# Order of the row loads of two engines in a graph layer: four rows a turn, semaphores in program order

## Chip, cores and metric

The kernel runs on one core of one Trainium2 chip. The metric is device time in microseconds of that core, the median of several runs.

## What is computed

A pre-norm graph layer with a residual, on 12500 nodes of 128 features and 200000 edges that are sorted by their target `dst`. All arrays are float32. Cut to what matters:

```python
z = relu(layernorm(x))                                # 12500 x 128
agg = segment_sum(z[src], dst) / max(deg, 1)          # deg: edges that end at a node
h = relu(agg @ Wg + z @ Ws + bg)                      # 128 -> 128
h = tanh(h @ W1 + b1)                                 # 128 -> 512
h = tanh(h @ W2 + b2)                                 # 512 -> 512
out = x + h @ W3 + b3                                 # 512 -> 128
```

## The kernel before

**Start.** The normalised rows of `x` are computed and written to a table `htab` in device memory (one row is 512 bytes). The indices are transposed, so that column `c` of `scol` holds the 128 sources of chunk `c`, and `dloc` their targets relative to a window of target nodes.

**Chunks.** The 200000 edges are 1563 chunks of 128 edges. Since the edges are sorted by target, a chunk's targets lie with near certainty in a window of 144 nodes around 8c. For a chunk, `add(c)` (L432) lets PE multiply the 128 gathered rows by a one-hot matrix `oh` (made by DVE for 8 chunks together, L382, with its column counts `cnt`, L392), which adds each row to its target's column of a PSUM accumulator `agg`. Chunks whose window reaches over two blocks are added in `edge`, copied out by ACT (`sums`) and merged by two further products. If an edge lay outside its window, a flag would send the program to a general version, which is not run here.

**Rows of a chunk** come in one of three ways:

- 1437 chunks by an indirect transfer of POOL from `htab` into one of 32 buffers (`gather`, L308). Up to 32 are asked for ahead of PE.
- 80 chunks (`raw`, 8 in each 40 from chunk 256 on to chunk 656) directly from `x`, at the start of the kernel, normalised afterwards in SBUF.
- 46 chunks (`slow`) by 128 single transfers of one row each, with the row's address from a register: 27 chunks (`slow_s`) by SP into the tiles `srows`, and 19 (`slow_a`) by ACT into `arows`. This is `row_loads` (L337), a generator: for 32 rows the addresses are loaded into registers, then 32 transfers are issued, and at each `yield` it hands back to the main loop. ACT's stops after four rows, SP's after 32. Each of the two has four tiles.

**Blocks.** The target nodes form blocks of 512 (64 chunks), smaller at the end. For block `b` the layers (`part0` to `part4`) follow when its chunks are added. `own` (L480) asks SP for the block's rows of `htab` (`hb`), and `own_turned` (L489) lets PE turn them by four transposes (`pt`) into `hT`, which ACT copies out. `own_part` asks SP for the rows of `x` (`xb`). `part4` leaves the result `o`, which `store` lets SP write out twelve chunks later (`LATE`), and without a delay from chunk 1376 (`QUICK`) on.

**Order.** The main loop runs over all chunks. PE's products, ACT's operations and the transfers of SP and ACT are kept in program order on their own engine by `tc.keep_in_program_order` (helpers at L297, L300, L306, L329, L332, L335). All else, the order between two engines included, is set by the scheduler, which lays all instructions out in one order by its estimate of their times. In that order the transfers of SP and ACT get eight completion semaphores in turn. A transfer waits until all earlier ones of its semaphore are done.

In the main loop the turn of the row loads is set by `behind`, the number of chunks gathered by POOL that have been passed:

```python
        if not raw(c) and c not in slow:
            behind += 1
            batch = behind * P // (EACH * LOADS)               # EACH = 48, LOADS = 32
            if behind > SLOW0 - 3 * EACH and batch > (behind - 1) * P // (EACH * LOADS):
                next(loading, 0)                               # SP: 32 rows each 12 chunks
            batch = behind * P // (EACH_A * TOGETHER)          # EACH_A = 60, TOGETHER = 4
            if behind > 48 and batch > (behind - 1) * P // (EACH_A * TOGETHER):
                next(loading_a, 0)                             # ACT: four rows each 1.9 chunks
```

A chunk loaded by rows is complete some 100 chunks before it is used. At `c % 64 == 54` come `own_turned` of the next block and right behind it `own` of the one after, so that `hb` is asked for 64 chunks ahead of its use.

Of the kernel before, what the change touches and what calls it, by code (L numbers as in the profile page):

```python
# [31 lines left out]
P = 128  # L32
# [9 lines left out]
SLOW0 = 160  # L42
EACH = 48
EACH_A = 60
TOGETHER = 4
LOADS = 32
# [14 lines left out]
def windowed(ctx, tc, x, src, dst, Wg, Ws, bg, W1, b1, W2, b2, W3, b3, out, flag):  # L61
    nc = tc.nc
# [19 lines left out]
    def raw(c):  # L82
        return RAW0 <= c < RAW1 and (c - RAW0) % STEP < GRP


    slow_s, slow_a = [], []
# [47 lines left out]
    for t, a in ((rsrc, src), (rdst, dst)):  # L134
        a = a[RAW0 * P : RAW1 * P].rearrange("(u e) -> u e", u=NRAW)[:, : GRP * P]
# [46 lines left out]
    def centre(pool, xt, k, stats):  # L182
        nc.vector.tensor_reduce(stats[:, 0], xt, AX.X, ALU.add)
        nc.vector.scalar_tensor_tensor(xt, spread(stats[:, 0], k), -1.0 / D, xt, op0=ALU.mult, op1=ALU.add)
        sq = pool.tile([P, k, D], F32, name=f"sq{k}")
        nc.scalar.activation(sq, xt, AF.Square)
        nc.vector.tensor_reduce(stats[:, 1], sq, AX.X, ALU.add)

    def factors(stats):
        nc.scalar.activation(stats[:, 1], stats[:, 1], AF.Sqrt, bias=eps, scale=1.0 / D)  # L190
        nc.vector.reciprocal(stats[:, 1], stats[:, 1])
# [110 lines left out]
    def flat(t):  # L302
        return t.rearrange("p a b -> p (a b)")

    def sp_dma(*a):
        tc.keep_in_program_order(nc.sync.dma_start(*a))  # L306

    def gather(c):  # L308
        r = rows_in.tile([P, D], F32, name="rows")
        nc.gpsimd.indirect_dma_start(  # L310
            out=r, out_offset=None, in_=htab,
            in_offset=bass.IndirectOffsetOnAxis(ap=scol[:, c : c + 1], axis=0),
        )
        rows_t[c] = r
# [10 lines left out]
    class act:  # L325
# [6 lines left out]
            tc.keep_in_program_order(nc.scalar.copy(*a))  # L332

        def dma(*a):
            tc.keep_in_program_order(nc.scalar.dma_start(*a))  # L335

    def row_loads(chunks, engine, dma, name, together):  # L337
        for c in chunks:
            i = slow.index(c)
            r = rows_one.tile([P, D], F32, name=name)  # L340
            rows_t[c] = r
            rb = r.bitcast(U8)
            for p0 in range(0, P, LOADS):
                loads, vs = nc.values_load_multi_w_load_instructions(  # L344
                    place[i : i + 1, p0 : p0 + LOADS], engines=[engine], min_val=0, max_val=(N - 1) * ROWB,
                    skip_runtime_bounds_check_because="src holds rows of x, as the indirect DMAs take it to",
                )
                for ld in loads:
                    tc.keep_in_program_order(ld)
                for p, v in enumerate(vs, p0):  # L350
                    dma(rb[p : p + 1, :], hbytes[bass.ds(v, ROWB)].rearrange("(o b) -> o b", o=1))
                    if (p + 1) % together == 0:
                        yield

    def raw_stats(i):
        return stats_raw[:, :, i * GRP : (i + 1) * GRP]

    def raw_scaled(i):
        h = raw_rows[i]
        scale(h, h, GRP, raw_stats(i))  # L360
        for j in range(GRP):
            rows_t[RAW0 + i * STEP + j] = h[:, j]
# [11 lines left out]
    def onehot(g):  # L374
        k = min(GRP, NCH - g * GRP)
        lo, w = window(g * GRP)
        is_raw = raw(g * GRP)
        oh = ed.tile([P, GRP, W_RAW], F32, name="ohr", bufs=2) if is_raw else oh_bufs[g % OHS]
        if not is_raw and w < oh_w[g % OHS]:
            nc.vector.memset(oh[:, :, w : oh_w[g % OHS]], 0.0)  # L380
            oh_w[g % OHS] = w
        nc.vector.tensor_tensor(  # L382
            oh[:, :k, :w], lane[:, None, :w].to_broadcast([P, k, w]),
            dloc[:, g * GRP : g * GRP + k][:, :, None].to_broadcast([P, k, w]), op=ALU.is_equal,
        )
        ohs[g] = oh
        step, n = (oh.shape[2], w) if is_raw else (PITCH - per, w + per * (k - 1))
        cnt = ed.tile([P, PITCH], BF16, name="cnt", bufs=16)
        part, row, col = oh.ap
        shifted = bass.AP(tensor=oh.tensor, offset=oh.offset, ap=[part, [col[0], n], [step * col[0], k]])  # L390
        with nc.allow_low_precision(reason="whole numbers up to the chunks of a group"):
            nc.vector.tensor_reduce(cnt[:, :n], shifted, AX.X, ALU.add)  # L392
        counts[g] = (lo, n, cnt)
# [10 lines left out]
    def count(b):  # L404

        n, m = blocks[b]
        dg = flat(ps_m.tile([P, 4, P], F32, name="pm"))
        groups = sorted({c // GRP for c in reach[b]})
        for g in groups:
            lo, w, cnt = counts[g]  # L410
            a0, a1 = max(lo, n), min(lo + w, n + m)
            pe.matmul(
                dg[:, a0 - n : a1 - n], ones, cnt[:, a0 - lo : a1 - lo], start=(g == groups[0]), stop=(g == groups[-1]),
                skip_group_check=True,
            )
        rd = ml.tile([P, BLK], F32, name="rd", bufs=3)
        nc.vector.tensor_scalar(rd[:, :m], dg[:, :m], 1.0, None, op0=ALU.max)  # L417
        nc.vector.tensor_reduce(total[:, b : b + 1], dg[:1, :m], AX.X, ALU.add)
        nc.vector.reciprocal(rd[:, :m], rd[:, :m])  # L419
        rds[b] = rd  # L420
# [189 lines left out]
        )  # L610

    order = [c for c in range(NCH) if not raw(c) and c not in slow]
    loading = row_loads(slow_s, mybir.EngineType.SP, sp_dma, "srows", LOADS)
    loading_a = row_loads(slow_a, mybir.EngineType.Activation, act.dma, "arows", TOGETHER)
    work, done, nxt, behind = [], 0, 0, 0
    ngrp = -(-NCH // GRP)
# [3 lines left out]
    def store(upto):  # L620
        while stores and stores[0][0] <= upto:
            sp_dma(*stores.pop(0)[1:])

    def soonest():
        two = work[: 2 if len(work) > 1 and work[1][3] < work[0][3] and work[0][4] else 1]
        return min(two, key=lambda w: max(w[2], now), default=None)
# [16 lines left out]
    for c in range(NCH):  # L643
        g = c // GRP
        at = c
        store(c if c >= QUICK else c - LATE)
        if c % GRP == 0 and g + 2 < ngrp:
            onehot(g + 2)
            if raw((g + 2) * GRP):
                raw_scaled(((g + 2) * GRP - RAW0) // STEP)  # L650
            if 2 <= g < 2 + NRAW:
                centre(ed, raw_rows[g - 2], GRP, raw_stats(g - 2))
            if g == 2 + NRAW:
                factors(stats_raw)

        while c % GRP == GRP // 2 and counted < len(blocks) and reach[counted][-1] // GRP <= g + 1:
            count(counted)
            counted += 1
        while nxt < len(order) and nxt < behind + AHEAD:
            gather(order[nxt])  # L660
            nxt += 1
        if not raw(c) and c not in slow:
            behind += 1
            batch = behind * P // (EACH * LOADS)
            if behind > SLOW0 - 3 * EACH and batch > (behind - 1) * P // (EACH * LOADS):
                next(loading, 0)
            batch = behind * P // (EACH_A * TOGETHER)
            if behind > 48 and batch > (behind - 1) * P // (EACH_A * TOGETHER):
                next(loading_a, 0)
        if c >= QUICK:  # L670

            there = 7.5 + 1.251 * (NRAW * GRP + order.index(c)) if c not in slow else 0
            while soonest() and max(now, soonest()[2]) < there:
                go_on(soonest())
            now = max(now, there) + 0.27
        add(c)

        lead = LEAD if c < QUICK else 2
        if done < len(blocks) and (c - lead if across[done] else c) >= reach[done][-1]:
            if across[done]:  # L680
                merge(done)
            quick = reach[done][-1] + LEAD >= QUICK

            before = done - 1 if done and reach[done - 1][-1] + LEAD < QUICK else None
            work.append([layers(done, before), 0, 0, 0, quick and blocks[done][1] <= P])
            done += 1

        if c % span == span - 10 and (c // span + 1) * BLK < N:
            own_turned(c // span + 1)
            if (c // span + 2) * BLK < N:  # L690
                own(c // span + 2)
        if c < QUICK:
            if c % 2 == 0:
                go_on(work[0] if work else None)
        if c == QUICK:
            for b, (_, n) in enumerate(blocks):
                if n < BLK:
                    own_part(b)
# [379 lines left out]
```

## Time and profile before

| | |
|---|---|
| runs (us) | 2780.86, 2771.82, 2799.8; median 2780.86 |
| profiled execution | 2780.86 us; span 2778.6 us from the first to the last instruction |
| mean clock of PE that was granted | 0.743 |
| busy, share of the span | PE 48%, PEld 32%, DVE 38%, ACT 8%, POOL 52% |
| POOL, gathers | 1437 of 945 ns each; first at 114.6 us, last at 2728.2 us |
| SP, row transfers | 3456; first at 117.0 us, last at 2654.4 us |
| ACT, row transfers | 2432; first at 217.8 us, last at 2330.1 us |
| PE, first and last chunk added | 118.0 and 2762.6 us |

Times are from one execution, and lines named L are lines of the kernel. SPq and ACTq are the engines as issuers of transfers; an issuing instruction does not count as busy, so SP has no busy time on the page. PEld is PE's load of the stationary operand, which runs beside its products. A line of waits reads: who waited, for whom, microseconds in total, times, longest. A line of the timeline reads: start, length, what, how many merged, and in brackets the idle time before it and what ended that.

### The profile page before, as it was taken

Reading aid. Unit: us, or ns where it says so; the run is one execution under the profiler, and the core shown is the slowest. Engines: PE = TensorE matmul, PEld = TensorE weight load, DVE = VectorE, ACT = ScalarE, POOL = GpSimd, SP = SyncE. Lnnn points to the kernel's source line nnn. Section 1 sums busy time; section 2 is a strip of 40 time slices with the busy share of each in tenths; the row PEclk is TensorE's granted clock in tenths of the full one; section 3 lists DMA queues with packets and bytes.
Section 4 is the critical chain, followed back from the end, with each engine's and each line's share of the span. In section 5 each row is a group of like instructions: output and inputs, shape, how many; then the busy total and the mean of one; then the engine's idle time right before and its main releaser. Section 6 shows DMA issues by size and latency. Waiting matters only on the chain. (4 is left out here: it accounts for less than half of the span.)

```text
span 2778.6 us, 27033 instructions
## 1 busy us (share of the span) xinstructions
PE 1321.2 (48%) x5212; PEld 886.9 (32%) x5212; DVE 1068.0 (38%) x651; ACT 228.0 (8%) x362; POOL 1437.0 (52%) x1525
## 2 busy tenths in 40 slices
PE   0233535445546564653525534355454453357167
PEld 0122323334324342332313323233232332224147
DVE  6834534254335343442414333243332432224141
ACT  1100100001000000000000000000000000001012
POOL 7666456554555444555526454364544545346261
PEclk9995767777767777786757777676676776678588
DMA  7511111111112111111111111111111111112120
GB/s 185 151 46 50 39 47 47 46 42 43 45 42 52 42 47 44 50 49 42 48 34 50 38 47 42 40 51 39 47 42 41 50 41 45 35 44 51 37 59 23
DMA packets 130516, 139.83 MB, mean 50 GB/s; under 512 B 35940, under 2 KB 105230, under 8 KB 130144
## 3 DMA queue, kind: packets, MB, share of 16 engines
q0 software_dynamic: 48544, 99.52, 14.2%
q1 hardware_dynamic: 73678, 33.92, 4.4%
q10 hardware_dynamic: 8116, 4.59, 0.7%
q14 instruction: 135, 1.11, 0.1%
q8 instruction: 43, 0.70, 0.1%
HBM read 125.07 MB, written 12.82 MB: 50 GB/s over the span
## 5 line engine op out<-in xcount | busy, mean ns | idle before, releaser
L310 POOL DMA_INDIRECT rows<-htab,scol x1437 | 1358.6, 945 | 1266.1 <-PE edge L297 441.5
L297 PE MATMUL pm<-h,w 128*128 128x512 f32 (+4 forms) x1344 | 732.0, 644 | 442.9 <-ACT h L329 237.1
L382 DVE TENSOR_TENSOR oh<-shared,dloc 128x1152 f32<-128x1152 f32 (+2 forms) x186 | 244.1, 1318 | 1203.8 <-PE edge L297 532.8
L392 DVE TENSOR_REDUCE cnt<-oh 128x200 bf16<-128x1600 f32 (+2 forms) x186 | 523.0, 2817 | 5.3
L297 PEld LDWEIGHTS agg<-oh,rows 128*128 128x128 f32 x2070 | 395.1, 236 | 323.4 <-issue 291.4
L297 PE MATMUL agg<-oh,rows 128*128 128x144 f32 (+3 forms) x2070 | 423.5, 336 | 76.0 <-issue 52.0
L297 PEld LDWEIGHTS pm<-h,w 128*128 128x128 f32 x1344 | 246.7, 226 | 478.2 <-ACT h L329 247.1
L300 PE MATMUL pt<-ident,hb 128*128 128x128 f32 x98 | 25.9, 409 | 543.2 <-DMA hb<-htab 480.3
L300 PEld LDWEIGHTS pt<-ident,hb 128*128 128x128 f32 x98 | 17.1, 208 | 548.1 <-issue 548.1
L297 PEld LDWEIGHTS edge<-oh,rows 128*128 128x128 f32 x804 | 146.3, 219 | 116.2 <-issue 113.5
L297 PE MATMUL edge<-oh,rows 128*128 128x144 f32 (+2 forms) x804 | 158.8, 316 | 16.9 <-issue 12.5
L329 ACT ACTIVATE h<-pm,b2c 128x512 f32<-128x512 f32 (+4 forms) x112 | 70.9, 633 | 722.8 <-DMA arows<-htab 224.2
L297 PE MATMUL pm<-mT,wg 128*128 128x512 f32 (+4 forms) x56 | 42.0, 843 | 143.8 <-DVE mT L533 91.5
L329 ACT ACTIVATE h<-pm,b1c 128x512 f32<-128x512 f32 (+4 forms) x112 | 69.8, 632 | 303.1 <-DMA arows<-htab 129.8
L589 DVE TENSOR_TENSOR o<-pt,xb 128x512 f32<-128x512 f32 x23 | 15.9, 691 | 202.7 <-PE pt L300 72.5
L153 POOL DMA_INDIRECT raw<-in_x_dram,rsrc x80 | 77.5, 969 | 25.4 <-issue 24.1
L297 PE MATMUL agg<-sums,ident 128*128 128x140 f32 (+4 forms) x108 | 25.3, 370 | 121.9 <-ACT sums L332 78.2
L419 DVE RECIPROCAL rd<-rd 128x512 f32<-128x512 f32 (+4 forms) x28 | 81.8, 2920 | 0.0
L417 DVE TENSOR_SCALAR rd<-pm 128x512 f32<-128x512 f32 (+4 forms) x28 | 17.4, 620 | 132.5 <-remote 61.8
L297 PEld LDWEIGHTS agg<-sums,ident 128*128 128x128 f32 x108 | 19.2, 243 | 126.2 <-ACT sums L332 79.8
L297 PEld LDWEIGHTS pm<-mT,wg 128*128 128x128 f32 x56 | 11.7, 259 | 148.1 <-DVE mT L533 94.2
L332 ACT COPY hT<-pt 128x512 f32<-128x512 f32 (+1 forms) x25 | 14.4, 578 | 541.4 <-PE pt L300 490.9
(72 smaller groups left out, 526.7 us busy)
## 6 DMA issues: line engine op xcount, KB each, us to landing
srows<-htab SPq DMA_DIRECT2D x3456, 0.5 KB
arows<-htab ACTq DMA_DIRECT2D x2432, 0.5 KB
rows<-htab,scol POOLq DMA_INDIRECT x1437
hb<-htab SPq DMA_DIRECT2D x24, 256.0 KB
xb<-in_x_dram SPq DMA_DIRECT2D x23, 256.0 KB
out_dram<-o SPq DMA_DIRECT2D x23, 256.0 KB
htab<-h SPq DMA_DIRECT2D x6, 896.0 KB
xt<-in_x_dram SPq DMA_DIRECT2D x5, 896.0 KB
```

What stands on the lines that cost most here:

```text
L153: nc.gpsimd.indirect_dma_start(out=t[:, j, :], out_offset=None, in_=x, in_offset=bass.IndirectOffsetOnAxis(ap=rsrc[:, g, j : j + 1], axis=0),)
L297: tc.keep_in_program_order(nc.tensor.matmul(*a, **k))
L300: tc.keep_in_program_order(nc.tensor.transpose(*a, **k))
L310: nc.gpsimd.indirect_dma_start(out=r, out_offset=None, in_=htab, in_offset=bass.IndirectOffsetOnAxis(ap=scol[:, c : c + 1], axis=0),)
L329: tc.keep_in_program_order(nc.scalar.activation(*a, **k))
L332: tc.keep_in_program_order(nc.scalar.copy(*a))
L382: nc.vector.tensor_tensor(oh[:, :k, :w], lane[:, None, :w].to_broadcast([P, k, w]), dloc[:, g * GRP : g * GRP + k][:, :, None].to_broadcas ...
L392: nc.vector.tensor_reduce(cnt[:, :n], shifted, AX.X, ALU.add)
L417: nc.vector.tensor_scalar(rd[:, :m], dg[:, :m], 1.0, None, op0=ALU.max)
L419: nc.vector.reciprocal(rd[:, :m], rd[:, :m])
L589: nc.vector.tensor_tensor(o[:, :whole], po[:, :whole], xb[:, :whole], op=ALU.add)
```

## The change

A helper `in_turn` takes the place of `tc.keep_in_program_order` for the transfers of `sp_dma` and of `act.dma`. Besides keeping each engine's own order it ties each transfer to the one before it in the program, on whichever of the two engines that was. The tie holds for the order in which the scheduler lays the instructions out, and so for the handing out of the semaphores; it adds no wait of its own. It covers the row loads of both engines and, on SP, `hb`, `xb`, the small blocks' rows of `x`, and the stores.

SP's row loads stop after each four rows (`TOGETHER`), and the loop takes a turn at two of three gathered chunks instead of at each twelfth. The address loads stay at 32 rows. The number of chunks, of rows, and the pace of rows per chunk stay.

```diff
+    turn = []
+
+    def in_turn(start):
+
+        tc.keep_in_program_order(start)
+        if turn:
+            tc.add_manual_dep(
+                start.ins, turn.pop(),
+                mybir.DependencyInfo(mybir.DependencyClass.NoSync, mybir.DependencyReason.DATA), reason="in_turn",
+            )
+        turn.append(start.ins.name)
+
     def sp_dma(*a):
-        tc.keep_in_program_order(nc.sync.dma_start(*a))
+        in_turn(nc.sync.dma_start(*a))
 ...
         def dma(*a):
-            tc.keep_in_program_order(nc.scalar.dma_start(*a))
+            in_turn(nc.scalar.dma_start(*a))
 ...
-    loading = row_loads(slow_s, mybir.EngineType.SP, sp_dma, "srows", LOADS)
+    loading = row_loads(slow_s, mybir.EngineType.SP, sp_dma, "srows", TOGETHER)
 ...
-            batch = behind * P // (EACH * LOADS)
-            if behind > SLOW0 - 3 * EACH and batch > (behind - 1) * P // (EACH * LOADS):
+            batch = behind * P // (EACH * TOGETHER)
+            if behind > SLOW0 - 3 * EACH and batch > (behind - 1) * P // (EACH * TOGETHER):
                 next(loading, 0)
```

## Prediction

> **What bounds the kernel now.** I read the page first, then the waits of PE, ACT and SP, then the timeline around one block, then the stretches of SP's row loads. The page shows no full engine: POOL 52%, PE 48%, DVE 38%.
>
> ```profile
> PE 1321.2 (48%) x5212; PEld 886.9 (32%) x5212; DVE 1068.0 (38%) x651; ACT 228.0 (8%) x362; POOL 1437.0 (52%) x1525
> ...
> L310 POOL DMA_INDIRECT rows<-htab,scol x1437 | 1358.6, 945 | 1266.1 <-PE edge L297 441.5
> ```
>
> The reader sees the gathers take 1.25 us each when they run back to back (0.945 and a 0.30 gap), which is 1437 x 1.25 = 1796 us of a span of 2778.6. The other 1000 us are waits, and POOL's own waits end with PE, because a gather reuses a buffer that PE has read. So the list of waits decides:
>
> ```profile
> PE pt L300 <- DMA hb<-htab: 480.3, 19, 45.1
> ...
> ACT h L329 <- DMA arows<-htab: 721.0, 88, 25.5
> ```
> ```profile
> SPq L306 <- DMA arows<-htab: 136.6, 114, 12.9
> SPq L306 <- DVE o L589: 73.9, 3, 49.0
> SPq L306 <- DMA srows<-htab: 54.3, 112, 1.4
> ```
>
> PE waits 480.3 us for `hb`, 19 times, some 25 us each. ACT's activations wait behind its row loads. SP itself waits for little. The order of time around one block shows why:
>
> ```profile
> 899.52 25.24 SPq L306 DMA_DIRECT2D srows<-htab  x58
> ...
> 924.86 0.41 SPq L306 DMA_DIRECT2D hb<-htab  x1
> 925.35 0.46 SPq L306 DMA_DIRECT2D out_dram<-o  x1
> ...
> 927.76 1.09 PE L300 MATMUL pt<-ident,hb 128*128 128x128 f32 x4 [12.40 <-DMA hb<-htab]
> ...
> 931.84 0.95 POOL L310 DMA_INDIRECT rows<-htab,scol  x1 [19.58 <-PE edge L297]
> ```
>
> SP issues 58 rows, then the `hb` load; PE has been idle for 12.40 us when that lands, and POOL for 19.58. In the program `own` places this load 64 chunks ahead of `own_turned`, which reads it. It arrives just too late, so **SP is about 64 chunks behind PE** at every block from about 640 us on.
>
> Why is SP late? Two stretches give its own price, one with POOL still and one with POOL at work and ACT's rows over (the last is issued at 2330.1):
>
> ```profile
> 2380.04 5.72 SPq L306 DMA_DIRECT2D srows<-htab  x18
> ...
> 2432.46 64.83 SPq L306 DMA_DIRECT2D srows<-htab  x96
> ```
> ```profile
> 2380.00:2385.80 5.80, 0.00 (x0) 0.00 (x0) 0.00 (x0) 0.00 (x0) 0.00 (x0) 0.50 0.01 2
> 2432.40:2497.30 64.90, 34.47 (x114) 19.30 (x112) 19.54 (x10) 6.66 (x10) 31.70 (x34) 0.74 0.14 36
> 640.00:2255.00 1615.00, 796.83 (x3058) 523.10 (x3058) 589.98 (x320) 117.11 (x180) 815.89 (x863) 0.72 0.17 44
> ```
>
> (Columns: stretch, length, then PE, PEld, DVE, ACT, POOL busy with instructions, clock, DMA.) With no gather a row costs 5.72/18 = 0.32 us; with 34 gathers 64.83/96 = 0.68. **A gather costs SP time.** In the long stretch 640 to 2255 SP issues 2241 rows, 70 register loads of 2.0 us and 45 large transfers of 0.45, beside 863 gathers, and waits 137 us for semaphores (101 for ACT's rows, 35 for its own). 1615 - 137 - 717 - 140 - 20 = 601, or 0.70 us per gather. The short stretch gives (64.9 - 30.7 - 4.0)/34 = 0.89. So SP is 91% occupied, and the 480 us at `hb` are mostly SP's lateness seen from PE.
>
> **The change, part by part.**
>
> Four rows a turn instead of 32. Nothing is added: 3456 rows, 27 chunks, register loads of 32 values as before. The pace is the same, 128/48 = 2.67 rows for each chunk that POOL gathers; the first rows stand at chunk 16 rather than 23. The `hb`, `xb` and store transfers have at most a few rows before them in one turn. Cost 0; at most 31 rows x 0.32 = 10 us of head start for one transfer, hidden while the program runs late.
>
> The order of the semaphores. Each transfer of SP and ACT waits for the semaphore that it will count up, one of eight handed out in turn, so it waits for the transfer eight places earlier in the laid-out order, whichever engine that is on. As built now, that order sets SP's row 960 (program chunk 432) beside ACT's row 827 (chunk 493): SP is planned 61 chunks late, and 62 to 74 at nearly every later point until ACT has no more rows. The lag is therefore held in place by semaphores; SP could not catch up. In the new order SP and ACT stand at the same chunk. `hb` is then issued about 64 chunks (over 100 us) before its use, and the 480.3 us go. What is late next is ACT: it can no longer be more than about eight transfers ahead of SP, an activation is queued behind each row load, PE waits for the activation and POOL for PE. So **PE goes at SP's pace**, without the 64 chunks of credit that it now draws between 200 and 640 us and pays back at the end.
>
> SP's pace per gathered chunk: 2.67 x 0.32 = 0.85 for rows, 2.67/32 x 2.0 = 0.17 for register loads, 0.02 for large transfers, 0.70 for the gather: 1.74 us, and 1.93 by the short stretch. I take 0.70, the longer stretch with both engines loading. To this comes SP's own waiting, not shown for the new order. From below it is 0. From above it is today's 8.5% in the long stretch and the longest waits (12.9 us once a block of 110): up to 15%. In the new order turns of four and four mostly repeat after eight, so that a transfer mostly waits for its own engine; the two meet where SP has two turns running, 10 to 8 over 15 chunks. I take 5%, giving 1.74/0.95 = 1.83. The measured pace now is 1615/863 = 1.87.
>
> Extra waits behind SP: a store now stands only 12 chunks after its block's last step, so it can wait for `o` with rows queued behind it. Today's worst is 73.9 us over three waits, near the end; 12 chunks are 22 us, which hide it. I add 0, and 24 x 3 us = 70 if not.
>
> The sum, on the profiled execution. Chunk 48, where ACT's rows begin, is added at 198 us and stays there. Chunks 48 to 1305 (the end of ACT's rows) hold 1138 gathered ones: 1138 x 1.83 = 2083, until 2281 (now 2295). Chunks 1305 to the last take 467 us now, with SP some 70 chunks late. Afterwards SP starts them level, and 332 of its rows are left. Bounds: POOL's 251 x 1.25 = 314, and today's 467. I take 370, or 1.47 a chunk, the pace of chunks 320 to 448 now (653 to 849 us is 1.53) slightly bettered. From the last chunk's product to the end 16 us stay. 198 + 2083 + 370 + 16 = 2667. The execution itself took 2780.86 us, 2.3 more than its span and equal to the median of the three times: **2670 us**.
>
> Two rules of the Trainium skill bear on this. "DMA: Bandwidth & Descriptors", section "Issuing engines are not separate DMA queues", says that the sequencer's time to start a transfer is usually small beside the transfer; by that SP would not be the limit, and the whole wait at `hb` would be won, 2781 - 480 = 2301. The rows above (0.68 us a row in issue alone) disagree, and decide. The same page, section "Rules for kernel authors", wants a semaphore dedicated to each use, which speaks against sharing eight between two engines: without sharing, the waiting share would be 0 and the sum 198 + 1980 + 370 + 16 + 2 = 2566.
>
> **The rivals.**
>
> A. Nothing to be measured: SP's pace with today's waiting, 1.74/0.915 = 1.90, and an end phase of 400: 198 + 2162 + 400 + 16 + 2 = 2778. For it: SP's work is the same, instruction for instruction. Against: the end phase is freed of the lag.
>
> B. Slower, by the lockstep. ACT and SP can no longer slide against each other, so SP, which is full, also waits whenever ACT stands behind an activation (ACT waits 167.5 us for `pm` of PE, 164.3 for `agg`). It decides where the pace passes (2781 - 2 - 198 - 370 - 16)/1138 = 1.93 us, that is SP waiting over 10%. At 15% the pace is 2.05: 198 + 2333 + 370 + 16 + 2 = 2919. For it: the 0.89 of the short stretch alone brings 1.93. Against: SP is the slowest of the two, so ACT should be found waiting, not SP.
>
> C. Large gain: the slow steps of SP come from the crossed semaphores and go with them. Then POOL sets the pace, near 1.4: 198 + 1593 + 340 + 16 + 2 = 2149. Against: 64.83 us for 96 rows with no row of ACT's about.
>
> D. That the semaphores stay interleaved as now: then `hb` still waits, and it is about 2780.
>
> **How the numbers follow.** Forecast (2500 to 2753) 0.55, C and all below 2500 0.08, A and D 0.11, B 0.26. From below: no waiting, 0.70, end phase 340: 198 + 1980 + 340 + 18 = 2536; C takes it lower. From above: B at 12%, 1.98 x 1138 + 586 = 2839. The range is 2480 to 2850. A measurement of this kernel (2771.82 to 2799.8) can tell about 1% from no change: faster 0.63, same 0.11, slower 0.26.
>
> **What would show it.** Right: PE's wait for `hb` below 50 us; SP's rows close to PE's chunk (row 2880 issued when PE is near chunk 1220 instead of 1299); ACT's wait behind row loads still the largest of all; the pace in the middle between 1.75 and 1.9 us per gather and SP's waits below 6%; chunks 1305 on in under 400 us. Wrong: a pace over 1.93, or SP's waits over 10%, gives B; a row of SP's at 0.32 us beside running gathers gives C; `hb` waits unchanged give D.

## Result, and the profile after

The kernel after takes 2655.11 us in the median (2637.8 to 2670.46), the kernel before beside it 2778.41: a ratio of 0.954, interval 0.946 to 0.962. A later repetition gave 2648.21 against 2769.27, 0.957 (0.953 to 0.961). Times of the kernel before in this text lie between 2755 and 2800 us. The one exception stands beside the run with no rows and half of the gathers: there it took 2012.02 us, so that run's time is compared with no other.

The profiled execution of the kernel after took 2670.46 us, with a span of 2667.5 and a clock of 0.753 (before: 0.743). Lines of the code have moved by 12. From the page, the engines and the gathers:

```profile
PE 1312.6 (49%) x5212; PEld 892.2 (33%) x5212; DVE 1069.0 (40%) x651; ACT 226.0 (8%) x362; POOL 1436.9 (54%) x1525
...
L322 POOL DMA_INDIRECT rows<-htab,scol x1437 | 1358.7, 946 | 1153.4 <-PE agg L297 468.7
```

The engines do the same number of operations in nearly the same busy time. What changed is who is waited for. PE's waits of the kernel after:

```profile
PE pm L297 <- ACT h L341: 487.0, 58, 53.9
...
PE pt L300 <- DMA hb<-htab: 35.7, 1, 35.7
```

The wait for `hb` fell from 480.3 us in 19 to 35.7 us in one. In its place stands PE's wait for ACT's activations, 487.0 us, and ACT waits behind its own row loads (all waits of the kernel after):

```profile
ACT h L341 <- DMA arows<-htab: 803.1, 96, 35.0
PE pm L297 <- ACT h L341: 487.0, 58, 53.9
POOL rows L322 <- PE agg L297: 468.7, 137, 40.3
ACT h L341 <- DMA srows<-htab: 443.0, 26, 28.3
```

The total of PE's longest wait has hardly changed; the time has, by 4.6%. So the 480 us were no sum to be won: they were SP's pace, seen at another place (the experiments below bear on this). SP's own waits in the whole run, and its timeline around one block:

```profile
SPq L318 <- DVE o L601: 81.1, 3, 58.5
SPq L318 <- DMA srows<-htab: 66.8, 141, 1.5
SPq L318 <- DMA arows<-htab: 11.4, 16, 2.8
```
```profile
1120.10 19.60 SPq L318 DMA_DIRECT2D srows<-htab  x19
1139.77 0.41 SPq L318 DMA_DIRECT2D hb<-htab  x1
1140.27 4.60 SPq L318 DMA_DIRECT2D srows<-htab  x8
1145.66 0.69 SPq L318 DMA_DIRECT2D out_dram<-o  x1
```

SP's waits for ACT's rows went from 136.6 us to 11.4. The `hb` issued there at 1139.77 us is read by PE at 1228.23, in a line that has no idle time before it:

```profile
1228.23 0.97 PE L300 MATMUL pt<-ident,hb 128*128 128x128 f32 x4
```

Between issue and use lie 88 us, and near 80 at most blocks; in the block of the kernel before that the prediction shows it was about three (924.86 to 927.76).

How late SP is can be counted for every row that it issues between 640 and 2255 us: the chunk that PE has reached, less the chunk at which the program asks for the row. That is 52 to 94 chunks before, and 1 to 26 after.

The middle stretch of the kernel after:

```profile
640.00:2255.00 1615.00, 825.98 (x3219) 551.52 (x3220) 630.24 (x342) 122.52 (x191) 860.65 (x911) 0.74 0.18 47
```

It holds 910 gathers of rows and 2418 row loads of SP (before: 863 and 2241). That is a pace of 1615/910 = 1.775 us a gather, where it was 1.871. SP's waits in this stretch, before and then after:

```profile
SPq L306 <- DMA arows<-htab: 101.5, 88, 10.1
SPq L306 <- DMA srows<-htab: 35.1, 77, 1.4
```
```profile
SPq L318 <- DMA srows<-htab: 49.0, 102, 1.5
SPq L318 <- DMA arows<-htab: 6.3, 10, 1.2
```

All waits together are 137 us before and 58 after. Take them off, and SP needs (1615 - 137)/863 = 1.71 us a gather before and (1615 - 58)/910 = 1.71 after. Call this SP's price. It did not change: in the middle the kernel won what SP no longer waits, and nearly all of that is waiting for ACT's rows.

Where the 111 us of span went, by the times at which PE adds a chunk:

| | before, us | after, us |
|---|---|---|
| until chunk 48 | 198.0 | 190.0 |
| chunks 48 to 320 | 455.1 | 492.0 |
| chunks 320 to 640 | 467.0 | 447.2 |
| chunks 640 to 1305 | 1175.3 | 1131.3 |
| chunks 1305 to the last | 467.2 | 389.6 |

Chunks 48 to 320 lose 37 us, since PE may no longer run ahead of SP on credit. From there to chunk 1305 the kernel wins 64 us, and in the end, which no longer pays the credit back, 78. The loss can be seen. SP's first 104 rows take 1.5 us each. ACT's rows, now tied to these, begin at 258.2 us and not at 217.8, and 68 of them then stand in one go before an activation:

```profile
115.22 156.09 SPq L318 DMA_DIRECT2D srows<-htab  x104
...
290.39 35.13 ACTq L347 DMA_DIRECT2D arows<-htab  x68
325.58 0.69 ACT L341 ACTIVATE h<-pm,bgc 128x512 f32<-128x512 f32 x1 [34.95 <-DMA arows<-htab]
```

PE's longest wait for ACT, the 53.9 us above, ends right after this activation. In the kernel before, SP's first 96 rows are as slow (151.78 us), but there PE did not have to wait for them. Why rows are that slow at the start stays open.

### The profile page after: what moved, and what is told of

Read it like the earlier page. It is cut to its first block, busy times and chain, and to the rows that moved or that the text cites. A ratio compares the mean times of both kernels' runs of the same rounds, so it can differ in the third digit from the quotient of the medians.

```text
span 2667.5 us, 27066 instructions
## 1 busy us (share of the span) xinstructions
PE 1312.6 (49%) x5212; PEld 892.2 (33%) x5212; DVE 1069.0 (40%) x651; ACT 226.0 (8%) x362; POOL 1436.9 (54%) x1525
## 5 line engine op out<-in xcount | busy, mean ns | idle before, releaser
L297 PEld LDWEIGHTS agg<-oh,rows 128*128 128x128 f32 x2070 | 382.9, 230 | 299.9 <-issue 279.7
L297 PE MATMUL agg<-oh,rows 128*128 128x144 f32 (+3 forms) x2070 | 406.2, 328 | 72.3 <-issue 63.3
L297 PEld LDWEIGHTS edge<-oh,rows 128*128 128x128 f32 x804 | 155.3, 229 | 133.3 <-issue 130.1
L297 PE MATMUL edge<-oh,rows 128*128 128x144 f32 (+2 forms) x804 | 169.9, 330 | 30.7 <-issue 28.0
L545 DVE TENSOR_TENSOR mT<-agg,rd 128x512 f32<-128x512 f32 (+4 forms) x28 | 17.4, 621 | 224.9 <-PE agg L297 166.7
L297 PE MATMUL pm<-cnt,ones 128*128 128x200 bf16 (+7 forms) x294 | 35.3, 285 | 125.9 <-issue 67.4
L341 ACT ACTIVATE h<-pm,b1c 128x512 f32<-128x512 f32 (+4 forms) x112 | 69.4, 632 | 319.8 <-DMA arows<-htab 165.0
L297 PEld LDWEIGHTS <-ones 128*128 128x128 bf16 x294 | 31.6, 129 | 132.5 <-issue 130.7
L300 PE MATMUL pt<-ident,hb 128*128 128x128 f32 x98 | 19.9, 331 | 74.0 <-issue 38.1
L341 ACT ACTIVATE h<-pm,bgc 128x512 f32<-128x512 f32 (+4 forms) x28 | 17.7, 633 | 422.9 <-DMA arows<-htab 189.1
```

The source lines that it names most:

```text
L297: tc.keep_in_program_order(nc.tensor.matmul(*a, **k))
L300: tc.keep_in_program_order(nc.tensor.transpose(*a, **k))
L341: tc.keep_in_program_order(nc.scalar.activation(*a, **k))
L545: nc.vector.tensor_tensor(mT[:, :n], acc[b][:, :n], rds.pop(b)[:, :n], op=ALU.mult)
```

## Experiments

**One half of the change: the order of the semaphores alone.** The tie between the two engines stays, SP issues 32 rows a turn again.

```diff
-    loading = row_loads(slow_s, mybir.EngineType.SP, sp_dma, "srows", TOGETHER)
+    loading = row_loads(slow_s, mybir.EngineType.SP, sp_dma, "srows", LOADS)
```

(and `LOADS` for `TOGETHER` in the two lines of its `batch`.)

> The new order of the semaphores, but SP's turn stays at 32 rows. Theory 1 (SP's issue pace is the bound; the order decides who waits for it): SP's planned lag against ACT is 0 to 1 chunks as in the changed kernel, so PE's wait for hb goes (below 60 us). But a turn of 32 rows fills the eight semaphores four times over, so ACT stands still for a whole turn (32 x 0.67 = 21 us each 12 chunks) and SP then waits until ACT has issued its six or seven turns: SP waits 10 to 20% and the pace is 1.74/0.85 = 2.05 us a gather, 2800 to 2950 us. Rival (the order is all of it, the size of the turn costs nothing): 2655 within 1%.

Measured: 2997.98 us, ratio 1.079 (1.074 to 1.084), above the expected 2800 to 2950. From its waits of all engines, and SP's:

```profile
ACT h L341 <- DMA arows<-htab: 1328.6, 122, 44.9
PE pm L297 <- ACT h L341: 854.4, 73, 62.3
```
```profile
SPq L318 <- DMA arows<-htab: 445.3, 132, 35.3
```

The order alone does take SP's lag away: `hb` is waited for once, 37.1 us, and chunks 1305 on take 382.9 us. But a turn of 32 rows of one engine uses up the eight semaphores four times over. The first transfers of the other engine's next turn then wait for the last of these, and so the engines go by turns. In the middle SP waits 300 of 1615 us, 18.6% (270.3 of them for ACT's rows), and the pace is 2.047 us a gather. SP's price is (1615 - 300)/789 = 1.67, so the loss is waiting. This is rival B of the prediction, and more than its 15%.

**The other half: four rows a turn alone,** in the kernel before, without the tie.

```diff
-    loading = row_loads(slow_s, mybir.EngineType.SP, sp_dma, "srows", LOADS)
+    loading = row_loads(slow_s, mybir.EngineType.SP, sp_dma, "srows", TOGETHER)
```

(with `EACH * TOGETHER` in `batch`.)

> Turns of four rows for SP, without the tie between the engines. In this program SP stays planned 68 to 74 chunks behind ACT, as before. Theory 1: hb still comes too late, PE waits for it 400 us or more, the pace in the middle stays at 1.87 us a gather: 2780 within 1.5%. Rival (long turns of SP block the hb load, and short ones free it): hb wait below 150 us and 2650 to 2700 us.

Measured: 2742.5 us, ratio 0.987 (0.981 to 0.992). The wait that the change was to remove is all there (PE's waits):

```profile
PE pt L300 <- DMA hb<-htab: 469.4, 19, 37.0
```

SP issues its rows in the middle 52 to 90 chunks late, as before. With the 1.3% go fewer waits of SP for ACT's rows, 69.4 us instead of 136.6, and an end of 455.5 us instead of 467.2. So the halves give +7.9% and -1.3%, and both together -4.6%: the order needs the small turns.

**Is it the lag itself, or `hb` that comes late?** The kernel before with `hb` asked for 128 chunks ahead instead of 64, and a third tile for it.

```diff
-        hb = ml.tile([P, BLK // P, D], F32, name="hb", bufs=2)
+        hb = ml.tile([P, BLK // P, D], F32, name="hb", bufs=3)
...
-            if (c // span + 2) * BLK < N:
-                own(c // span + 2)
+            if (c // span + 3) * BLK < N:
+                own(c // span + 3)
```

(`own(2)` is added at the start, and `cnt` has 15 tiles instead of 16 to make room.)

> The kernel before, with hb asked for 128 chunks ahead instead of 64 (three hb tiles, and 15 instead of 16 cnt tiles to make room). Theory 1: PE's wait for hb was only where SP's lateness came to light; with hb earlier SP is planned some 100 chunks behind ACT instead of 65, the end of the kernel has to wait for it all the same, and the time stays between 2700 and 2790 us, the waits moving to the rows or to ACT. Rival theory 2 (the late hb itself is what the change cured): the 480 us go and the time is that of the changed kernel or less, 2660 us or below.

Measured: 2782.94 us, ratio 1.001 (0.998 to 1.003). Nothing is won, though PE's wait for `hb` is down to 36.9 us, once. PE now waits for SP's chunks, and DVE for `xb`, which SP loads too (PE's waits, then DVE's):

```profile
PE agg L297 <- DMA srows<-htab: 191.2, 8, 34.1
```
```profile
DVE o L589 <- DMA xb<-in_x_dram: 302.0, 15, 65.7
```

SP used the longer leash and fell 63 to 123 chunks behind in the middle; the pace is 1.846 us a gather, the end 485.6 us. The wait at one tile was a symptom: with a full engine behind it, asking earlier moved the wait.

**SP's price with nothing to cross.** The kernel after with SP's 27 chunks and none of ACT's; POOL gathers the 19.

```diff
-        elif na <= 0 and c < QUICK + EACH_A:
+        elif na <= 0 and c < 0:
```

> The changed kernel with SP's 27 chunks kept and ACT's 19 given to POOL: no semaphore is shared between two engines' row loads. Theory 1: SP stays full, at 1.74 us a gather, but ACT is no longer held by it, and PE may again run 64 chunks (hb) ahead: SP's last row near 117 + 1296 x 1.74 = 2372, the end 2450 to 2600 us. Rival (the crossing of two engines is the bound): the 2309 us of the kernel without rows.

Measured, one run: 2654.7 us, beside 2758.8 of the kernel before. The middle goes at 1615/930 = 1.737 us a gather. SP still waits 45 us of it, for its own rows; its price is 1.69, where the prediction had 1.74. With no ACT rows to hold PE back, SP again falls behind, 52 to 91 chunks in the middle, `hb` is waited for and the end takes 436.0 us. So the lag needs no crossing of semaphores: a full SP is enough, and it goes on until PE waits for `hb`. PE's waits and SP's:

```profile
PE pt L300 <- DMA hb<-htab: 603.1, 18, 52.1
```
```profile
SPq L318 <- DMA srows<-htab: 64.9, 137, 1.4
```

The run missed its range, 2450 to 2600, from above: SP's last row came at 2504.7 us and not near 2372. The expectation gave every row the price of the middle, but the first 648 rows, those of 243 gathers, took until 640 us, or 2.1 us a gather. The rival (the crossing of the engines is the bound, 2309) falls: without any crossing SP is just as full.

In the eight profiles here that have SP's 27 chunks and all gathers, the pace in the middle lies between 1.737 and 2.047 us a gather, and SP's price, its waits taken off, between 1.67 and 1.74.

**The same with fewer or no rows.** ACT's 19 chunks alone, then 14 chunks of SP (`EACH` = 96) beside ACT's, then none (`SLOW0` = 2000).

```diff
-        if ns <= 0:
+        if ns <= 0 and c < 0:
```

> The changed kernel with ACT's chunks kept (20 of them) and SP's given to POOL. Theory 1: ACT needs 2.13 x 0.33 + 0.15 for rows and 0.2 for its own operations, and some 0.4 for the gathers, 1.45 us a gather in all; that is the pace of the kernel without rows, so 2310 to 2450 us. Rival (row loads in ACT's queue, in front of activations, are the drag): 2550 us or more.

```diff
-EACH = 48
+EACH = 96
```

> The changed kernel with SP's chunks cut from 27 to 14 (each 96th chunk), ACT's 19 kept. Theory 1: SP's price falls to 0.43 + 0.08 + 0.02 + 0.70 = 1.23 us a gather, below the 1.44 us that the kernel without rows keeps, so the time comes near that kernel's 2309: 2300 to 2450 us. Rival (the lockstep of the two engines holds the pace): 2600 us or more.

```diff
-SLOW0 = 160
+SLOW0 = 2000
```

> The changed kernel with no chunk loaded by rows: the 46 chunks go to POOL, which then gathers 1483. Theory 1: SP and ACT are free, POOL sets the pace at 1.25 us: 111 + 1483 x 1.25 + 50 = 2015, and with some waits of PE 2000 to 2120 us. Rival (the lockstep and the chain of layers hold the pace, the row loads only share the blame): 2400 us or more.

Measured: 2344.22 us for ACT alone, 2354.13 for half of SP's (one run each), and 2308.58 with no rows, ratio 0.830 (0.827 to 0.833); a repetition of the last gave 2301.32. It is **the fastest kernel here that computes the whole**. The pace in the middle is 1.482, 1.495 and 1.443 us a gather. Each chunk that SP takes off POOL costs more than POOL needs for it: 2655 less 2344 us over 27 chunks is some 11 us a chunk, and a gather takes POOL 1.25. Row loads in ACT's queue are not the drag: with ACT's chunks alone the time is near that of no rows. The end takes 387.8 us without any row and 389.6 in the kernel after, which speaks for rows no longer holding the end.

The run without rows missed its range, 2000 to 2120: gathers back to back (1.25 us) do not set its pace. Its waits of PE's weight loads:

```profile
PEld agg L297 <- issue: 429.2, 881, 5.8
```

These weight loads waited 429.2 us for nothing that the profile shows; in the kernel after it is 347.7 us.

**Is it the gathers that slow SP?** The kernel after, with every second gather left out: the next chunk is computed from the same rows.

```diff
     def gather(c):
+        if len(shared_rows) == 1:
+            rows_t[c] = shared_rows.pop()
+            return
...
+        shared_rows.append(r)
```

> The changed kernel, but POOL gathers only every second of its chunks, and the chunk after it is added from the same rows (the sums are so computed from other rows; the row loads and all else stay). Theory 1: a gather takes 0.70 us from SP, so SP's price of a gathered chunk falls from 1.74 to 0.85 + 0.17 + 0.02 + 0.35 = 1.39 us, and the time to 190 + 1138 x 1.45 + 360 + 17 = 2200 to 2350 us. A row of SP's costs some 0.5 us. Rival (SP's slow steps have nothing to do with POOL): the row stays at 0.67 us and the time at 2600 us or more.

Measured, one run: 1986.37 us, 28% under the kernel before beside it and below the expected 2200 to 2350. Against the kernel after, from which it was made, it is some 25% (2655 us, on another occasion). SP's rows are the same 3456 and POOL was not full. From one row's start to the next, all steps under 2 us from 640 us on (to 2255 us, and to 1900 with half the gathers), by the number of gathers that start between 2.5 us before the step and 0.5 us after its start:

| mean step of SP, us | 0 | 1 | 2 | 3 |
|---|---|---|---|---|
| before | 0.354 | 0.431 | 0.686 | 0.778 |
| after | 0.359 | 0.453 | 0.659 | 0.795 |
| half the gathers | 0.370 | 0.388 | 0.469 | 0.480 |

The mean over all these steps is 0.56 us in the kernel after and 0.42 with half the gathers. At 2.67 rows a chunk that is 0.37 us; between chunks 640 and 1305 the pace fell by 0.48, from 1.762 us to 1.279 for each chunk with gathered rows. So most of what half the gathers give back is SP's issue time. It is not PE's work that slows SP's rows: with half the gathers PE is busy for 66% of the stretch and not 51%, and the rows are cheaper. That a step beside two gathers is cheaper too, 0.469 for 0.659, is more than the count of gathers explains, and stays open.

**What holds the kernel without rows?** Both at once: no rows, and half of the gathers.

> The kernel after without any row load, and POOL gathers only at every second of its chunks; the next chunk is computed from the same 128 rows instead of its own. It asks why the run without row loads went at 1.44 us a gather and not at the 1.25 us of gathers back to back, with PE marked as idle for nothing shown (its issue). Theory: the gathers themselves hold PE's own issue up, as they hold up SP's rows; with half of them the middle goes well below 1.25 us a chunk, and the whole to 1650 to 1900 us. Rival: PE, with what it waits for from ACT and DVE, has a pace of its own of about 1.44 us a chunk that no gather causes: then the time stays near 2309 us (2200 to 2350). In between, about 1.25 us a chunk and 2050, would leave it open.

Measured, one run: 1212.88 us, below all that was expected, on the occasion when the kernel before took 2012.02. A stretch of the middle (length; PE, PEld, DVE, ACT, POOL busy; clock):

```profile
300.00:900.00 600.00, 594.94 (x3006) 410.35 (x3005) 580.36 (x321) 112.72 (x175) 407.42 (x432) 1.00 0.24 68
```

PE is busy for 99% of it, at the full clock, and 0.63 us a chunk between chunks 640 and 1305. It is inconclusive: the gathers, the clock (1.00, and 0.77 in the middle of the run with all gathers) and the occasion changed together, and any of them can have shortened the waits for nothing shown.

**The same kernels again,** to see how far that occasion reaches.

> The kernel after, unchanged, beside the kernel before, because the kernel before took 2012 us in the last call and 2759 to 2800 us in the ones ahead of it. Theory: SP's row issue is what such a chip has less of to pay, and the change is worth the less the less SP is the limit: where the kernel before takes near 2012 us, the kernel after is within 2% of it; where it takes near 2780, the ratio is 0.95 again. Rival: the wait at hb costs the same share everywhere, and the ratio is 0.94 to 0.965 at 2012 us too (1890 to 1940 us).

> The kernel before, unchanged, for a profile on the same chip as the kernel after. If it takes near 2012 us: the theory expects a row of SP beside two or three gathers at 0.45 us or less instead of 0.69 to 0.75, SP's lag behind PE the same 60 to 80 chunks or less, and PE's wait for hb under 150 us; the rival expects rows at 0.69 and another engine or wait to have given back the 770 us. If it takes near 2780 us, nothing new is expected of it.

> The kernel after without any row load, as before, on the same chip. At a granted clock near 0.8 it takes 2309 us and 1.44 us a gather again. Theory, if the chip is the one on which the kernel before took 2012 us: PE's issue waits are small there and the pace is that of gathers back to back, 1.25 us, 1900 to 2050 us. Rival: the pace of 1.44 belongs to the gathers and stays, 2250 to 2320 us.

Measured: 2648.21 us, 2763.57 and 2301.32, all near their first times, so what their expectations say of 2012 us could not be tried. The readings repeat: `hb` is waited for 476.2 us before; the pace is 1.867 us a gather before and 1.748 after, the end 457.2 and 372.9 us. Why the kernel before once took 2012 us stays open. By the account given here SP's row loads would have been cheaper then, but no profile with rows was taken on that occasion. The run with no rows and half of the gathers was the only experiment on its chip; the others ran on three more. Whether the chip makes the difference was not tried.

## Why the prediction was right

The forecast case came true by its own steps: SP stayed the bound, the wait for `hb` went, SP's waiting shrank and the end was freed of the lag. The sizes are near, and some of the nearness is luck.

- **Start.** 198 us was put in for the first 48 chunks; 190.0 came.
- **SP's pace as the bound.** Forecast 1.83 us a gather for chunks 48 to 1305; they took 2070.5/1138 = 1.82. That is the mean of two misses: 1.96 from chunk 48 to 320, where the sum had no term for SP's slow first rows, and 1.78 from 320 on. SP's price was read a little high: 1.71 in the kernel after and 1.69 in the run with SP alone, against 1.74.
- **SP's waiting.** 5% were taken, 58 of 1615 us or 3.6% came, and 49.0 of the 58 us are waits for SP's own rows. ACT's rows cost 6.3 us. Chunks 48 to 1305 took 2070.5 us instead of 2083.
- **The lag and `hb`.** Row 2880 was issued with PE at chunk 1235, not at 1299; the sign named was near 1220. SP was 1 to 26 chunks behind its place, `hb` came some 80 us ahead of its use and not over 100, and the wait was 35.7 us, under the 50 named. One reading goes too far: that the lag of the kernel before was held in place by semaphores. The run with SP alone has the same lag with no row of ACT's to cross.
- **ACT held by SP.** ACT's wait behind row loads is the largest of all, as said, and the credit of the time from 200 to 640 us was lost, as said. The sum gave this little weight: 251 gathers x 1.83 = 459 us for chunks 48 to 320, where 492.0 came.
- **The end.** 370 us were estimated, 389.6 measured (372.9 in the repetition), and 17 us from the last chunk instead of 16. The sum erred by 8 + 12 to the high side and by 20 + 1 to the low, which cancel: it gave 2667 us for the profiled execution, whose span is 2667.5. That is luck; the median lies 15 us lower.
- **Stores.** SP's waits for `o` went from 73.9 to 81.1 us, still three waits, none of them in the middle stretch: the zero held.

**The rivals.** A (today's waiting remains) falls with 3.6% for 8.5%. B (lockstep) is real but belongs to turns of 32 rows; with four rows SP was not caught. C (the slow steps come from the crossing) falls by the table of steps: beside two gathers 0.686 us before, 0.659 after. With no row of ACT's at all the mean step is 0.54 us, and 0.56 in the kernel after. D (the order stays interleaved) falls with the wait for `hb`.

**The two rules weighed.** The Trainium skill, "DMA: Bandwidth & Descriptors", section "Issuing engines are not separate DMA queues", takes the time to start a transfer for usually small. Here, with transfers of one row at 0.56 us from one to the next, SP's issue and its waits set the pace in every profile with its 27 chunks and all gathers, and about 2301 us were not reached by removing a wait but only by removing the rows. The same page's section "Rules for kernel authors" has for transfers "Dedicate one sem". No run here gave each use its own. What sharing cost SP itself in waits for ACT's rows in the middle was 6.3 us with small turns in program order and 270.3 with turns of 32 rows in the same order. Nearest to no sharing is the run with SP alone: 2654.7 us, where the prediction's sum without sharing gave 2566.

## What to carry to other kernels

When a wait names a late transfer, ask how full its issuer is before asking for the transfer earlier: with SP 91% occupied, an earlier request gave 1.001, and taking work off SP gave 0.83. Where two engines share completion semaphores in turn, the laid-out order binds them at run time. Lay it out level, and keep the turns short: beside eight semaphores, four rows a turn gave 0.954 and 32 rows 1.079; what lies between was not tried. Compare what a helper engine pays per unit with what the main engine would pay, measured with both at work: SP's row took 0.36 us with no gather near and 0.66 to 0.80 beside two or three.

## What the runs showed of the hardware that was not expected

- Gathers of POOL slow SP's row issue (0.36 us a row with none near, 0.66 beside two). Leaving out every second one took some 25% off the kernel after, although POOL had been busy for only 54% of its span.
- With no rows at all, POOL does not reach the 1.25 us of gathers back to back but goes at 1.44; PE's weight loads then wait 429.2 us for nothing that the profile shows. Whether that comes from the gathers or from the granted clock was not separated.
- One occasion gave the kernel before in 2012.02 us at a mean clock of 0.835 instead of some 2770 at 0.743 to 0.762; the cause is open. So a ratio is taken between runs of the same occasion.
